# A head's 16 values on every other partition in a two-layer attention kernel: q, k and sums moved without filler, heads from chip to chip, the denominators alone by way of DRAM

## The chip, the cores and the metric

The kernel runs on one core of one Trainium2 chip. The metric is device microseconds (us) of one execution. The kernel before took 2535.94 us, the median of three runs (2533.43 to 2537.54).

The profile calls the engines PE (TensorE, matrix products; PEld is its loading of weights), DVE (VectorE), ACT (ScalarE), POOL (GpSimd) and SP (SyncE, which here only issues DMAs). The matrix engine writes to PSUM, which is divided into banks; the other on-chip memory is SBUF, with 128 partitions.

## The reference

The input x has the shape (2, 2048, 256), in fp32: 2 sequences of 2048 tokens. There are two layers of the same form, and both read the same normalized input:

```
xn = layernorm(x)
s  = attention(xn)              # layer 0: softmax over all 2048 keys; + xn
                                # layer 1: only keys with |i - j| <= 64
g  = silu(ffn(xn))              # layer 0: two branches of 8 low-rank experts
                                # layer 1: a product and 8 gated LoRA experts
x  = x + s * g
```

Each attention has 16 heads of 16 values:

```
q, k, v = split(xn @ w_qkv + b_qkv)
attn    = softmax(q k^T * scale)   # scale 1/16 in layer 0, 1/4 in layer 1
heads   = attn v
s       = heads @ w_o + b_o        # layer 0 adds xn
```

## The kernel before, in words

**Storage.** All activations are kept transposed: the 256 features lie on partitions, as 2 halves (NC = 2) of 128, and the tokens lie along the free dimension, worked on in blocks of TB = 512. So a sequence (batch b) has NB = 4 blocks. The 16 heads form NG = 4 groups g of four heads. One *item* of attention is (b, g, n): a sequence, a group of heads and a block of 512 queries; there are 32 items in each layer.

**Stages, by the trace.** Products of weights and the first layer norm (0 to 57 us), the router (to 124), the first feed-forward part (to 471), the keys, queries and values of layer 0 and the start of its attention (to about 597), the attention of layer 0 (to about 2124), then the layer norm, the second feed-forward part and the keys and queries of layer 1 (to about 2225), the values of layer 1 and the start of its attention (to 2290), its attention (to 2505) and a tail.

**Keys and queries by way of DRAM.** `keys_queries` (L473) writes k and q of a block into the DRAM tensor `qd` (L195), which has HP = 32 rows for each head: 16 rows of values and 16 rows of filler. The filler is written once near the start (L301 to L310): a tile of ones and a tile of zeros, each 128x512, go out in eight DMAs, so that the filler rows of k are ones and those of q are zeros. `fetch` (L581) reads one (b, g) of k and q back, 128 partitions by 2048 tokens each, so that head j of the group stands on partitions 32j to 32j + 31. Two k tiles and two q tiles take turns. In layer 1 the fetch is cut into two halves. `attention` begins with the fetch of the first two groups.

**Two passes over the scores.** `scores` (L596) issues both passes, for four heads side by side: each head uses 32 rows of PE (32x128 weights), so four heads fill its 128 rows.
- The first pass (`sq`, L667) makes q·k for the row maximum only; DVE reduces it (L679 in layer 0; L674 with the band's mask in layer 1).
- The negated maximum is then put into row 16 (HD) of each head of the q tile, where k has a one. In layer 0 `turn_max` and `fetch_max` do so through the DRAM tensor `md` on SP's queue. In layer 1 `place_max` transposes the maxima on PE, negates them on ACT (`row<-pmx`, L723) and issues `q<-row` on ACT's own queue (L726).
- The second pass (`sk`, L667) then yields q·k minus the maximum; ACT takes the exponential (L683), and in layer 1 POOL sets to zero what lies outside the band (L688).

**Weighing the values.** `values` (L526) makes v for 128 tokens at a time: two matmuls into a PSUM bank of a pool of six (`pp`, L541), then a copy into the tile `vs[b]`, by DVE for the first sequence, by ACT for the second. POOL has filled that tile with ones before (L514). A head has HV = 17 columns there: 16 values and a one that remains. `weigh` (L733) takes a window of 32 columns a head, so that the accumulator `acc` (L747) holds, on partition 32j + 16, the sum of the exponentials of head j: the softmax's denominator. In layer 0 ACT copies acc away and POOL adds it to `av` (L760, L761); in layer 1 ACT copies it into `av` (L752).

**After an item.** When its `av` (128x512) is complete, six steps follow, each a number of attention steps after the other (the `hops`, L867):
- `away` (L771): all of av, 256 KB, goes to the DRAM tensor `ad`.
- `compact` (L779): the denominators come back as `dn`, 128x16, and the heads, 128 KB, come back into xn, whose values are no longer needed (both read `ad`).
- `invert` (L785): DVE takes the reciprocal of dn.
- `write` (L788): dn goes to DRAM, `rd`.
- `spread` (L791): it comes back as `recb`, each denominator repeated on the 16 partitions of its head.
- `divide` (L798): the multiplication of heads and recb, on POOL; in layer 1 every second item on DVE.

The last item of layer 0 and the last four of layer 1 take another way without DRAM (`last_there` L805, `last_back` L819: transposes on PE). `project` (L830) follows when all four groups of a block are done. In xn the heads of a group stand as (value, head): partition 4d + j of the group's 64. To match this, the host permutes rows of w_o and the bias of v (`apart` in `_attn_arrays`, L1122).

**What sets the order.** The order of everything in attention is written out by hand, in steps. A step of layer 0 is one key block of 128 and one query block of 512 for four heads, there are 512 of them; a step of layer 1 is two query tiles of 128, there are 64. `after` is a table that says which functions follow which step, and the loop at L945 issues in each step: the second pass of step s together with the first pass of step s + U + LEAD, then jobs left from the values and keys of the second sequence, the weighing of an earlier step, and the functions of the table. `pin` (L698) keeps an instruction at its place in the program order of its engine. Before this loop stand, without pins, the memsets of the tiles (L514 to L523, all on POOL), the values of the first sequence (L545) and the fetches. All of SP's DMAs pass its one queue in order.

```
hops = (0, 1, 3, 4, 5, 7, 8) if local else (0, 2, 4, 5, 7, 11, 13)
...
for hop, f in zip(hops, steps):
    at(end + DEL + hop, f, i)
```

## Time and profile before

| | |
|---|---|
| median of three runs | 2535.94 us |
| the profiled execution | 2538.34 us |
| its span, on the profile's page | 2536.6 us |
| around the span | 1.74 us |
| mean TensorE clock granted | 0.999 |
| bytes of all DMAs | 129.83 MB in 146353 packets, of which 93456 under 512 B |
| read from and written to HBM | 80.50 MB and 45.97 MB |
| L679, DVE maxima of layer 0 | 1024, 1221 ns each |
| L674, DVE maxima of layer 1 | 512, 410 ns each on average |
| L683, ACT exponentials of layer 0 | 2048, 603 ns each |
| L761, POOL additions of layer 0 | 459, 1267 ns each |
| L771, DMAs away from av | 59 of 256 KB |
| L783 and L796, DMAs of heads and of reciprocals | 59 of 128 KB each |
| L589, fetches of k and q | 10 + 10 of 1024 KB, and halves in layer 1 |

The profile is of one execution, and its times are in us unless ns is written. A group's line gives the code line, the engine, the operation, what it writes and reads with shapes, and how often; after it come busy time, mean ns of one, and the engine's idle time before these instructions with what released it. "Chain" is the chain of work that ended last. Lines of a timeline begin with the start from the span's beginning and the length of a row of like instructions; in brackets stands the idle time before it and what ended it.

### The profile page before, as it was taken

How to read it: one execution, taken by the hardware profiler on the slowest of the kernel's cores; microseconds unless marked ns; L12 is line 12 of the kernel's file. 1: busy time of each engine (PE TensorE's matmuls, PEld its weight loads, DVE VectorE, ACT ScalarE, POOL GpSimd, SP SyncE). 2: the span in 40 equal slices, each digit the busy share in tenths (PEclk: the TensorE clock that was granted, in tenths of full speed). 3: DMA queues.
4: the chain of work that ended last, by engine and by line, in shares of the span. 5: the costliest groups of instructions: out<-in, count | busy, mean ns of one | idle time of the engine just before them, and what ended most of it. 6: DMA issues, size and time to landing. Idle time of an engine off the chain costs nothing.

```text
span 2536.6 us, 47898 instructions
## 1 busy us (share of the span) xinstructions
PE 2513.1 (99%) x18896; PEld 1060.6 (42%) x18896; DVE 1686.2 (66%) x2747; ACT 1620.8 (64%) x3187; POOL 876.6 (35%) x827
## 2 busy tenths in 40 slices
PE   8999999999999999999999999999999999999999
PEld 6444444444333333333333333333333334457766
DVE  4143333157888888888777788788888765238986
ACT  5400000126888888888888888888888886227755
POOL 0000000102444444444444444444444420016887
PEclk9999999999999999999999999999999999999999
DMA  6131111230001001001001001001000002133552
GB/s 243 50 84 51 52 51 39 82 118 14 14 14 43 16 12 44 16 12 44 16 12 43 10 18 44 12 17 43 15 14 10 14 14 63 49 133 108 163 167 81
DMA packets 146353, 129.83 MB, mean 51 GB/s; under 512 B 93456, under 2 KB 97936, under 8 KB 143568
## 3 DMA queue, kind: packets, MB, share of 16 engines
q1 hardware_dynamic: 144256, 125.46, 16.5%
q8 instruction: 148, 2.42, 0.4%
q10 hardware_dynamic: 1872, 1.31, 0.2%
q14 instruction: 77, 0.63, 0.1%
HBM read 80.50 MB, written 45.97 MB: 50 GB/s over the span
## 4 chain that ended last, share of the span: by engine, by line
PE 79%; DMA 1%; ACT 0%; POOL 0%; DVE 0%; issue 0%; ACTq 0%; SPq 0%; POOLq 0%; DVEq 0%
PE sk L667 25%; PE acc L747 22%; PE sq L667 19%; PE pp L477 5%; PE pr L835 2%; PE pp L532 2%; PE po L1027 1%; PE pt L1023 1%; PE po L1035 1%; PE xb L113 0%; PE xb L138 0%; DMA k<-qd 0%; PE of L827 0%; DMA q<-qd 0%; POOL xn L688 0%
## 5 line engine op out<-in xcount | busy, mean ns | idle before, releaser
L679 DVE TENSOR_REDUCE part<-sq 128x2 f32<-128x1024 f32 x1024 | 1207.3, 1221 | 294.3 <-PE sq L667 284.7
L683 ACT ACTIVATE e<-sk 128x512 f32<-128x512 f32 x2048 | 1058.3, 603 | 217.2 <-PE sq L667 197.7
L667 PE MATMUL sk<-q,k 32*128 32x512 f32 (+2 forms) x5632 | 1135.8, 533 | 1.2 <-ACT xn L683 1.0
L667 PE MATMUL sq<-k,q 32*128 32x512 f32 (+2 forms) x5120 | 1129.1, 569 | 0.5 <-DVE part L679 0.5
L761 POOL TENSOR_TENSOR av<-av,more 128x512 f32<-128x512 f32 x459 | 581.4, 1267 | 936.3 <-ACT more L760 931.1
L667 PEld LDWEIGHTS sk<-q,k 32*128 32x128 f32 x5632 | 522.0, 184 | 604.1 <-ACT e L683 512.5
L747 PE MATMUL acc<-e,v 128*32 128x512 f32 x4096 | 546.7, 605 | 0.0
L667 PEld LDWEIGHTS sq<-k,q 32*128 32x128 f32 x5120 | 402.3, 183 | 22.3 <-DVE part L679 13.2
L760 ACT COPY more<-acc 128x512 f32<-128x512 f32 x459 | 268.7, 585 | 1.2 <-PE acc L747 1.0
L747 PEld LDWEIGHTS acc<-e,v 128*32 128x32 f32 x4096 | 81.8, 108 | 388.2 <-ACT e L683 367.8
L461 ACT ACTIVATE gt<-po 128x512 f32<-128x512 f32 x16 | 8.8, 594 | 321.1 <-PE po L457 321.1
L674 DVE CUSTOM_DVE_ANT_0 seen<-sq,mask 128x256 f32<-128x256 f32 (+1 forms) x512 | 176.2, 410 | 53.6 <-PE sq L667 49.2
L467 POOL TENSOR_TENSOR x<-x,up 128x512 f32<-128x512 f32 x16 | 23.1, 1461 | 450.1 <-DVE up L464 277.5
L448 DVE TENSOR_TENSOR xs<-we,px 128x512 f32<-128x512 f32 x64 | 43.9, 686 | 136.2 <-PE px L440 130.3
L688 POOL TENSOR_SCALAR_AFFINE_SELECT xn<-xn 128x512 f32<-128x512 f32 x172 | 106.2, 652 | 77.4 <-ACT xn L683 75.7
L440 PE MATMUL px<-xn,FV 128*128 128x512 f32 x256 | 121.2, 595 | 0.0
L444 PE MATMUL py<-cum,FW 128*128 128x512 f32 x256 | 120.5, 593 | 0.6 <-DVE cum L412 0.6
L424 PE MATMUL po<-pr,UO 128*128 128x512 f32 x256 | 119.0, 592 | 0.0
L683 ACT ACTIVATE xn<-sk 128x512 f32<-128x512 f32 x172 | 89.8, 602 | 41.1 <-PE sk L667 17.9
L450 DVE TENSOR_TENSOR pr<-xs,py 128x512 f32<-128x512 f32 x64 | 44.0, 687 | 64.8 <-PE py L444 64.6
L424 PEld LDWEIGHTS po<-pr,UO 128*128 128x128 f32 x256 | 48.6, 190 | 61.2 <-issue 61.0
L444 PEld LDWEIGHTS py<-cum,FW 128*128 128x128 f32 x256 | 48.4, 190 | 61.5 <-issue 59.8
(195 smaller groups left out, 1604.0 us busy)
## 6 DMA issues: line engine op xcount, KB each, us to landing
we<-wd SPq DMA_DIRECT2D x128, 128.0 KB
ad<-av SPq DMA_DIRECT2D x59, 256.0 KB
qd<-sb SPq DMA_DIRECT2D x48, 256.0 KB
k<-qd SPq DMA_DIRECT2D x10, 1024.0 KB
q<-qd SPq DMA_DIRECT2D x10, 1024.0 KB
xn<-ad SPq DMA_DIRECT2D x59, 128.0 KB
recb<-rd SPq DMA_DIRECT2D x59, 128.0 KB
q<-qd SPq DMA_DIRECT2D x12, 512.0 KB
```

The costliest lines, as they stand in the source:

```text
L424: nc.tensor.matmul(po[oc], UO[:, ch, bass.ts(oc, P)], pr, start=(ch == 0), stop=False)
L440: nc.tensor.matmul(px, FV[:, c, bass.ts(ch, P)], xn[b][:, c, cols], start=(c == 0), stop=(c == NC - 1))
L444: nc.tensor.matmul(py, FW[:, c, bass.ts(ch, P)], cum[:, c, :], start=(c == 0), stop=(c == NC - 1))
L477: nc.tensor.matmul(ps, w[:, c, bass.ts(hf, P)], xn[b][:, c, bass.ts(n, TB)], start=(c == 0), stop=(c == NC - 1))
L667: nc.tensor.matmul(o, lhs, rhs, start=True, stop=True)
L674: nc.vector.tensor_tensor_reduce(seen[:, lo:hi], sq[:, d, t * 2 * P + lo : t * 2 * P + hi], mask[:, lo:hi], 1.0, LOWEST, ALU.add, ALU.max, ...
L679: nc.vector.tensor_reduce(pt[:, pair[0] : pair[1] + 1, t, kb], sq, AX.X, ALU.max)
L683: nc.scalar.activation(e, t, AF.Exp, scale=scale)
L688: nc.gpsimd.affine_select(out=e[:, :, c, :], in_=e[:, :, c, :], compare_op=ALU.is_ge, fill=0.0, base=0, pattern=[[0, 4], [sign, P]], chann ...
L747: nc.tensor.matmul(acc[hp[j], o : o + hi - lo], vs[b][:, kt, vcols(g, j)], es[j][:, lo:hi], start=(r == 0), stop=(r == len(parts) - 1), sk ...
L760: nc.scalar.copy(more, acc)
L761: nc.gpsimd.tensor_tensor(avs[i], avs[i], more, ALU.add)
```

## The change

A head's 16 values now stand on the even partitions of its 32, and what stood on partition 16 moves to an odd one: the maximum's row of q is partition 31 (HP - 1) of each head, and the denominator is on partition 15 (DEN).

- `qd` holds 16 rows a head and no filler; the eight DMAs of filler and the tile of zeros are gone. `fetch` reads 64 rows into every second partition, half the bytes.
- The filler is made in SBUF: DVE sets both k tiles (2048 columns in layer 0, 2176 in layer 1) to one and both q tiles (2048 columns) to zero at the beginning of each attention.
- The first pass uses 31 rows a head, without the maximum's row; the second pass still 32.
- The copy of the values writes every second column of a head's window; the odd columns of the window are written by its two neighbours, except one, column 15, which keeps its one and gives the denominator on partition 15.
- `away` moves only the four denominators' rows, 8 KB. The heads no longer pass DRAM: `compact` moves them straight from av (every second partition) to xn, so av is released there, and no longer by `away`.
- dn is 32x64 instead of 128x16, and `rd` is read with the head as its outermost dimension (4) instead of the value (16).
- The heads stand in xn as (head, value), so `last_there` and `last_back` change their layout and the host no longer permutes w_o and the bias.

The instructions of PE keep their order and number, and so do the steps and hops.

```
+DEN = HD - 1
...
-        [2, B, H, HP, T], F32, name="qd"
+        [2, B, H, HD, T], F32, name="qd"
...
-        zeros = fw.tile([P, TB], F32, name="zeros")
-        nc.vector.memset(zeros, 0.0)
-        for b in range(B):
-            for i, t in ((0, ones), (1, zeros)):
-                for half in range(NC):
-                    nc.sync.dma_start(
-                        out=qd[i, b, bass.ts(half, H // NC), HD:, :], in_=t[:, None, :].to_broadcast([P, NB, TB])
-                    )
...
+            for k, q in zip(ks, qs):
+                nc.vector.memset(k, 1.0)
+                nc.vector.memset(q, 0.0)
             for t in vs:
                 nc.gpsimd.memset(t, 1.0)
...
+                s = vs[b][p0:p1, c, :]
                 copy(
-                    vs[b][p0:p1, c, : H * HV].rearrange("p (h w) -> p h w", w=HV)[:, :, :HD],
+                    bass.AP(s.tensor, s.offset, [s.ap[0], [HV, H], [2, HD]]),
                     ps[p0:p1, :].rearrange("p (h w) -> p h w", w=HD),
                 )
...
+            hq = [slice(j * HP, (j + 1) * HP - 1) for j in range(NG)]
...
-                    nc.sync.dma_start(out=t[:, to], in_=qd[i, b, bass.ts(g, NG), :, s].rearrange("h w t -> (h w) t"))
+                    nc.sync.dma_start(out=t[::2, to], in_=qd[i, b, bass.ts(g, NG), :, s].rearrange("h w t -> (h w) t"))
...
-                                        q1[hp[j], bass.ts(qt, P)], k1[hp[j], qt * P + lo : qt * P + hi],
+                                        q1[hq[j], bass.ts(qt, P)], k1[hq[j], qt * P + lo : qt * P + hi],
...
-                    out=q[HD:P:HP, bass.ts(n, TB)].rearrange("j (t c) -> j t c", c=P), in_=row
+                    out=q[HP - 1 : P : HP, bass.ts(n, TB)].rearrange("j (t c) -> j t c", c=P), in_=row
...
-                pin(nc.sync.dma_start(out=ad[i % 3].rearrange("j w f -> (j w) f"), in_=avs.pop(i)))
+                pin(nc.sync.dma_start(out=ad[i % 3], in_=avs[i][DEN::HP]))
...
-                return d.rearrange("j (r e) -> r j e", r=P // NG)
+                return d.rearrange("j (r e) -> (j r) e", e=DE)
...
-                divs[i] = op.tile([P, NG * TB // P], F32, name="dn", tag="dn", bufs=3)
-                pin(nc.sync.dma_start(out=divs[i], in_=flat(ad[i % 3][:, HD, :])))
-                pin(nc.sync.dma_start(out=together(*items[i]), in_=ad[i % 3][:, :HD, :].rearrange("j d f -> d j f")))
+                divs[i] = op.tile([NG * TB // DE, DE], F32, name="dn", tag="dn", bufs=3 if local else 1)
+                pin(nc.sync.dma_start(out=divs[i], in_=flat(ad[i % 3])))
+                pin(nc.sync.dma_start(out=together(*items[i]), in_=avs.pop(i)[::2]))
...
-                pin(nc.sync.dma_start(out=divs[i], in_=rd[i % 3][None, :, :].to_broadcast([HD, NG, TB])))
+                pin(nc.sync.dma_start(out=divs[i], in_=rd[i % 3][:, None, :].to_broadcast([NG, HD, TB])))
```

More of the change, by code (lines that the diff above doesn't have):

```diff
@@ L481, in keys_queries @@
         nc.scalar.activation(sb, ps, AF.Identity, bias=bias[:, hf : hf + 1])
-        nc.sync.dma_start(out=qd[i, b, bass.ts(hf, H // NC), :HD, bass.ts(n, TB)], in_=sb)
+        nc.sync.dma_start(out=qd[i, b, bass.ts(hf, H // NC), :, bass.ts(n, TB)], in_=sb)
     def attention(A, scale, local, final, start=None, projected=False):
@@ L501, in attention @@
         LEAD = 3 if local else 6
+        DE = 64
         DEL = 2 if local else 1
@@ L508, in attention @@
             ks = [kq.tile([P, T + 2 * PAD], F32, name=f"k{i}", tag=f"k{i}") for i in range(2)]
-            ad = [dr.tile([NG, HP, TB], F32, name=f"ad{i}", tag=f"ad{i}") for i in range(3)]
+            ad = [dr.tile([NG, TB], F32, name=f"ad{i}", tag=f"ad{i}") for i in range(3)]
             rd = [dr.tile([NG, TB], F32, name=f"rd{i}", tag=f"rd{i}") for i in range(3)]
             md = [dr.tile([NG * TT, P], F32, name=f"md{i}", tag=f"md{i}") for i in range(2)]
+            for k, q in zip(ks, qs):
+                nc.vector.memset(k, 1.0)
+                nc.vector.memset(q, 0.0)
             for t in vs:
@@ L663, in scores @@
                                 pieces.append((
-                                    when, sq[:, d], q1[hp[j], bass.ds(n1 * TB + t * P, P)], k1[hp[j], bass.ts(kb, TB)]
+                                    when, sq[:, d], q1[hq[j], bass.ds(n1 * TB + t * P, P)], k1[hq[j], bass.ts(kb, TB)]
                                 ))
@@ L709, in fetch_max @@
                 pin(nc.sync.dma_start(
-                    out=tiles(i)[0][HD:P:HP, bass.ts(items[i][2], TB)],
+                    out=tiles(i)[0][HP - 1 : P : HP, bass.ts(items[i][2], TB)],
                     in_=md[i % 2].rearrange("(j t) p -> j (t p)", t=TT),
@@ L810, in last_there @@
                     nc.tensor.transpose(ps[:, t].rearrange("p j w -> p (j w)"), av[:, bass.ts(t, P)], ident)
-                rec = op.tile([P, TT, NG], F32, name="dn", tag="dn", bufs=3)
-                o = divs[i] = op.tile([P, TT, HD, NG], F32, name="over", tag="recb", bufs=2)
-                nc.vector.reciprocal(rec, ps[:, :, :, HD])
+                rec = op.tile([P, TT, NG], F32, name="rec", tag="rec", bufs=2)
+                o = divs[i] = op.tile([P, TT, NG, HD], F32, name="over", tag="recb", bufs=2)
+                nc.vector.reciprocal(rec, ps[:, :, :, DEN])
                 nc.vector.tensor_tensor(
-                    o.rearrange("p t d j -> p t j d"), ps[:, :, :, :HD],
-                    rec[:, :, :, None].to_broadcast([P, TT, NG, HD]), ALU.mult,
+                    o, ps[:, :, :, ::2], rec[:, :, :, None].to_broadcast([P, TT, NG, HD]), ALU.mult
                 )
@@ L822, in last_back @@
                 lo = g % 2 * NG * HD
-                o = divs.pop(i).rearrange("p t d j -> p t (d j)")
+                o = divs.pop(i).rearrange("p t j d -> p t (j d)")
                 ps = pm.tile([P, TB], F32, name="of", tag="m")[lo : lo + NG * HD, :]
@@ L1122, in _attn_arrays @@
 def _attn_arrays(l, wq, wk, wv, bq, bk, bv, wo_t, bo):
-    apart = lambda m: m.reshape(NG, NG, HD, -1).transpose(0, 2, 1, 3).reshape(m.shape)
     cols = lambda v: np.asarray(v).reshape(NC, P).T
@@ L1129, in _attn_arrays @@
         f"wv{l}": wv,
-        f"wo{l}": apart(np.asarray(wo_t).T),
+        f"wo{l}": np.asarray(wo_t).T,
         f"bq{l}": cols(bq),
         f"bk{l}": cols(bk),
-        f"bv{l}": cols(apart(np.asarray(bv))),
+        f"bv{l}": cols(bv),
         f"bo{l}": cols(bo),
```

## The prediction

> **What bounds the kernel now.** I read the page's busy times and its chain first, then the busy time by stage, then the order of time at the two places where the change puts something new.

> ```profile
> span 2536.6 us, 47898 instructions
> PE 2513.1 (99%) x18896; PEld 1060.6 (42%) x18896; DVE 1686.2 (66%) x2747; ACT 1620.8 (64%) x3187; POOL 876.6 (35%) x827
> PE 79%; DMA 1%; ACT 0%; POOL 0%; DVE 0%; issue 0%; ACTq 0%; SPq 0%; POOLq 0%; DVEq 0%
> ```

> TensorE is idle for 23.5 us of the span and carries the chain. A busy PE can still be a slow PE, so I took the spacing of the acc groups of L747: in layer 0, 455 of some 500 steps are 2.92 or 2.93 us apart. A step holds three groups of eight matmuls (sk, sq, acc), each about 1 us. That is PE's own pace, not another engine's. By stage:

> ```profile
> 1200.00:1500.00 300.00, 300.00 (x2371) 101.87 (x2364) 237.80 (x222) 247.85 (x488) 133.06 (x105) 1.00 0.08 19
> 2225.00:2290.00 65.00, 64.17 (x281) 39.86 (x281) 21.84 (x99) 17.37 (x34) 9.63 (x10) 1.00 0.39 130
> 2290.00:2400.00 110.00, 108.25 (x2130) 86.60 (x2133) 98.10 (x553) 82.13 (x184) 88.56 (x138) 1.00 0.46 142
> 2400.00:2505.00 105.00, 103.20 (x1810) 75.92 (x1806) 85.62 (x444) 67.90 (x155) 88.18 (x126) 1.00 0.46 142
> ```

> Columns after the length: PE, PEld, DVE, ACT, POOL, then clock, DMA share, GB/s. Layer 0 leaves PE no idle time and DMA nearly none to do. In layer 1 (from 2290) PE is idle for 1.75 and 1.8 us only, but DVE is at 89% and DMA at 46%. So a transfer saved can bring back at most 3.55 us there, and DVE is the engine nearest to taking over. Before it, from 2225, lies a stretch in which PE fills PSUM banks that DVE must empty.

> **The change, part by part.**

> *The eight fills and the zeros tile.* They issue from 33.5 to 67 us. SP's next transfer is at 116.4, PE waits for a DMA only once early (4.7 us, before the fills), and it is busy for 63.00 of the 63 us after 64. I take 0; with no such cover, 0.5 us of gain.

> *Memsets of k and q, layer 0.* They go between the two last up steps at 470.9 (L464). DVE's next work is the first copy of values at 501.71, after 29.4 us of idle time, and some 9 us of memsets fit. Behind the second up waits POOL's add, then POOL's two memsets of v (474.70, 7.8 us); 2 us later is still before 501. I take 0.

> *The same memsets, layer 1.* Here there is no such gap.

> ```profile
> 2224.44 1.61 DVE L1041 SCALAR_TENSOR_TENSOR x<-gt,bo,x 128x512 f32<-128x512 f32 x2 [4.23 <-ACT gt L1039]
> 2224.75 8.27 POOL L515 MEMSET v<- 128x4879 f32 x2 [91.76 <-PE po L1035]
> 2225.32 15.23 PE L532 MATMUL pp<-wv,xn 128*64 128x256 f32 x68 [0.69 <-ACT gt L1039]
> 2228.95 2.43 DVE L535 COPY v<-pp 64x256 f32<-64x256 f32 x6 [2.89 <-POOL v L515]
> 2231.81 0.43 DVE L535 COPY v<-pp 128x256 f32<-128x256 f32 x1 [0.44 <-PE pp L532]
> ```

> PE runs 17 groups of values 0.865 us apart and has six banks. The six copies that wait for POOL until 2228.95 are just in time: the seventh group began at about 2231.8 - 0.9 = 2230.9 and needs the first copy's bank. In the changed program DVE does: x step, memset k (2176 columns), x step, memset q (2048), k, q, and only then the copies. The first k waits for PE's last po, so it starts near 2225.2. The rest is 0.8 us of x step and 8448 columns. What does a column cost?

> ```profile
> 1.27 0.48 DVE L302 MEMSET ones<- 128x512 f32 x1
> 1.82 0.48 DVE L305 MEMSET zeros<- 128x512 f32 x1
> ```

> The row says 485 ns for 512 columns, and with the mask's 272 ns for 256 that is 0.83 ns a column. The starts lie 0.55 us apart, 1.07 ns a column. [...] By the row the memsets take 7.0 us, the first copy ends at 2225.2 + 0.8 + 7.0 + 0.4 = 2233.4 and PE stands for 2.5 us. [...] I take 4.3, since starts show what the next instruction waits for. After it the copies run at 0.4 us against 0.865, so no second stall; but PE is full until 2290, so nothing gives the 4.3 back. [...] The trace's clock is 1.00 in every stage after the first, so I take 0 and keep 1.7 for the range.
> The fetches of k and q (SP) now wait for these memsets, until about 2227 to 2235 instead of 2224.7; they are half as large and first used at 2248. Behind them on SP is nothing until 2243.9. 0.

> *The first pass on 31 rows.* The tile stays 32x128 at the same place. The nearest row is L457 with 16 rows: 587 ns at least, like the 592 of the 128-row matmuls with 512 columns. I take 0. Each 10 ns a step would be 5 us, so this is a rival.

> *The reciprocal on 32x64 instead of 128x16, 59 times.*

> ```profile
> L786 DVE RECIPROCAL dn<-dn 128x16 f32<-128x16 f32 x59 | 14.4, 244 | 0.2
> L191 DVE RECIPROCAL rec_r<-mx_r 128x32 f32<-128x32 f32 x2 | 0.7, 354 | 0.1
> L191 DVE RECIPROCAL rec_g<-mx_g 128x16 f32<-128x16 f32 x2 | 0.5, 253 | 0.1
> ```

> 16 further columns cost 101 ns, so 64 columns cost 354 + 202 = 556 ns, 0.31 us more. In layer 0 (31 of them) DVE has 19% idle time: 0. In layer 1 (28) an item is 6.50 us of PE; DVE needs 16 x 0.344 + 0.25, and in every second item 0.85 for the division: 5.75 or 6.6 us, with 0.31 more 6.1 or 6.9. At one such item (2458) DVE left the second pair's bank 0.06 us before PE wrote it, so 0.25 us is lost. Fourteen items divide on DVE, four of them beside projections with room: 10 x 0.15 = 1.5 us taken; bounds 0 and 14 x 0.31 = 4.3.

> *Smaller transfers, layer 1.* Per item 256 KB out and 128 KB back become 8 KB out and 128 KB on the chip; fetches are halved. What they cost now:

> ```profile
> 2467.25 0.26 ACT L723 ACTIVATE row<-pmx 16x128 f32<-16x128 f32 x1
> 2468.87 0.54 ACTq L726 DMA_DIRECT2D q<-row  x1
> ```

> ACT held its queue for 1.3 us behind a fetch issued at 2463.97, and PE's acc came 1.18 us late. All layer 1 steps beyond 6.50 us an item add up to 2.5 us. I take -2.0; bounds -3.55 (all PE idle time) and 0. The later release of av (after the heads' move) has three buffers, 19.5 us, against some 11 us: 0.

> *The spread of the reciprocals.* Its source loses 16 as its outermost dimension and gets 4. [...] The write ahead of it lands sooner behind smaller fetches, so I take 0.

> *SP in layer 0.* The write of the maxima loses its wait for PE (16 waits, 6.4 us in all), but 9.94 to 11.08 us lie between its two DMAs, mostly the first one's landing. Six steps are late by 3.6 us in all. I take 0, bound -3.6. The away, compact and spread steps run tens of us ahead of need: 0.

> **Sum.** 4.3 + 1.5 - 2.0 = +3.8. The profiled execution took 2538.34 us (span 2536.6, 1.7 around it), so 2542.1 for such a one; it stands 2.4 above the median 2535.94, so against the median 2539.7, said as 2540. About 0.2%, 5.1 us, is what a measurement can tell from none.

> **Rivals.**
> - *Transfers were worth more* (faster). Layer 1's 3.55 us and layer 0's 3.6 all come back, the stall is only 2.5, the reciprocal hides: -4.7, 2531. For it: every such wait passes SP or a fetch. Against: layer 0's waits are for an unchanged DMA. Chance 0.13.
> - *DVE takes over layer 1* (slower). Once DVE's item is longer than PE's 6.50 us, each of the 14 dividing items passes on its 0.31 us, and PE's late start hides the transfers' gain: 4.3 + 4.3 = +8.6, 2544.5. For it: DVE's 89%. Against: items without a division have 0.4 us of room to catch up. Chance 0.28.
> - *The change does not do what it says: 31 rows cost.* If the four heads no longer ran side by side, eight matmuls of 0.59 us would replace a 1.07 us group, milliseconds in all. Chance 0.03.
> - The likeliest, 0.56: 2537 to 2543.

> It lies within 0.2% (up to 2541.0) in about three quarters and above in a quarter; 0.02 of each of the first two rivals ends within too. So same is 0.42 + 0.04 = 0.46, slower 0.14 + 0.26 + 0.03 = 0.43, faster 0.11. The range takes in the first rival's inner part and the clock beside the second: 2533 to 2548.

> **What would show it.** Right: sq groups as long as before and steps of 2.92; four DVE memsets ahead of the first v copy near 2234, with a gap of 3 to 5 us inside the values; reciprocals near 556 ns; no held q<-row at the fetches. Wrong: a gap under 2 us, layer 1 items well off 6.50 us, or a clock below 1.00 after the gap.

## The result and the profile after

The changed kernel takes 2544.94 us, the median of seven runs (2542.17 to 2548.56), beside 2536.73 us for the kernel before in seven runs (2532.11 to 2539.51). The ratio is 1.0035 with a 95% interval of 1.0025 to 1.0045: slower by some 8.9 us by the ratio; the two medians lie 8.2 us apart. That lies inside the range of the prediction, but above its likeliest case.

The head of the page of the changed kernel:

```profile
span 2543.5 us, 47862 instructions
PE 2517.2 (99%) x18896; PEld 1062.1 (42%) x18896; DVE 1716.5 (67%) x2754; ACT 1622.9 (64%) x3187; POOL 877.8 (35%) x827
DMA packets 119829, 89.68 MB, mean 35 GB/s; under 512 B 81160, under 2 KB 85640, under 8 KB 118324
```

The bytes moved fell from 129.83 to 89.68 MB, and PE's idle time rose from 23.5 to 26.3 us. But PE's busy time rose as well, by 4.1 us, with the same 18896 matmuls. That is a first hint of a slower clock somewhere. The same stages as before (length, busy times of PE, PEld, DVE, ACT and POOL, clock, DMA share, GB/s):

```profile
1200.00:1500.00 300.00, 300.00 (x2368) 102.40 (x2364) 238.79 (x221) 247.50 (x486) 132.95 (x105) 1.00 0.05 11
2225.00:2290.00 65.00, 60.32 (x257) 36.89 (x257) 24.77 (x87) 16.00 (x29) 7.80 (x10) 0.97 0.28 98
2290.00:2400.00 110.00, 108.68 (x2037) 85.98 (x2036) 99.33 (x542) 80.10 (x179) 83.68 (x131) 1.00 0.23 71
2400.00:2505.00 105.00, 104.42 (x1792) 76.31 (x1793) 91.81 (x462) 66.48 (x151) 86.67 (x126) 1.00 0.26 85
```

The second row is the boundary: PE's idle time went from 0.83 to 4.68 us, and the clock from 1.00 to 0.97. In layer 1 DMA is half as busy, DVE more, and PE counts as idle for 1.90 us instead of 3.55 although the stage takes longer: its waits for DVE apparently lie within its groups of matmuls and are not counted there, an inference from these two numbers and the longer items below. There the spacing of the items has to be read, not the busy time.

For the place of the time I took, from PE's order of time in both traces, the start of the first instruction of each kind:

| stretch | before | after | difference |
|---|---|---|---|
| start to the first product of the router (L329, L321) | 57.36 | 54.72 | -2.64 |
| to the first keys of layer 0 | 413.96 | 413.96 | 0.00 |
| to the first values of layer 1 | 1754.00 | 1754.82 | +0.82 |
| to the keys of the second sequence | 15.74 | 21.87 | +6.13 |
| to the first sq of layer 1 | 7.07 | 7.06 | -0.01 |
| to the first transposition of the tail | 253.92 | 256.51 | +2.58 |
| to the end of the span | 34.55 | 34.56 | +0.01 |

The sum is the 6.9 us between the two spans. The -2.64 us at the start is not the change's: two executions of the kernel before differ there by as much (last section). Without it the change costs +9.5 us in this pair of traces, of which 6.1 us lie in the values of layer 1, 2.6 us in its attention and 0.8 us in layer 0.

**The boundary.** The order of time there:

```profile
2222.93 8.27 POOL L512 MEMSET v<- 128x4879 f32 x2 [91.73 <-PE po L1032]
...
2223.50 5.59 PE L529 MATMUL pp<-wv,xn 128*64 128x256 f32 x24 [0.69 <-ACT gt L1036]
2223.78 1.87 DVE L509 MEMSET k<- 128x2176 f32 x1 [0.40 <-DVE x L1038]
...
2226.57 1.76 DVE L510 MEMSET q<- 128x2048 f32 x1 [0.38 <-issue]
...
2228.74 1.87 DVE L509 MEMSET k<- 128x2176 f32 x1 [0.40 <-issue]
...
2230.98 1.76 DVE L510 MEMSET q<- 128x2048 f32 x1 [0.37 <-issue]
...
2232.78 2.70 DVE L533 COPY v<-pp 64x256 f32<-64x256 f32 x7
2233.26 10.19 PEld L529 LDWEIGHTS pp<-wv,xn 128*128 128x128 f32 x40 [4.58 <-DVE v L533]
2233.26 11.60 PE L529 MATMUL pp<-wv,xn 128*128 128x256 f32 x44 [4.17 <-DVE v L533]
```

PE fills its six banks with 24 matmuls (four in each) and stands for 4.17 us, until the first copy. The four memsets and the x step between them take from 2223.78 to 2232.78. Then 44 matmuls take 11.60 us; at the pace of before (15.23 us for 68) they would take 9.86. So 1.74 us more are lost behind the gap. PE's granted clock in short stretches says why (length, PE busy, clock, DMA share, GB/s):

```profile
2229.10:2233.20 4.10, 0.00 (x0) 1.00 0.71 204
2233.20:2234.20 1.00, 0.94 (x3) 0.72 0.75 246
2234.20:2236.20 2.00, 2.00 (x6) 0.50 0.60 221
2236.20:2237.20 1.00, 1.00 (x4) 0.58 0.12 49
2237.20:2238.20 1.00, 1.00 (x6) 1.00 0.00 0
```

The clock is halved for some 3.4 us after PE starts again (3.41 us in the record of the clock, from 2233.63 on).

**Layer 1.** The reciprocals and divisions on DVE from 2290 to 2510:

```profile
L784 DVE RECIPROCAL dn<-dn 32x64 f32<-32x64 f32 x27 | 14.5, 536 | 0.2
L800 DVE TENSOR_TENSOR xn<-xn,recb 64x512 f32<-64x512 f32 x12 | 10.3, 862 | 0.5 <-DMA recb<-rd 0.3
```

A reciprocal went from 246 to 536 ns. Where it hurts is an item that also divides on DVE; one of these, in the kernel before and in the changed one:

```profile
2401.66 0.90 DVE L802 TENSOR_TENSOR xn<-xn,recb 64x512 f32<-64x512 f32 x1
2402.49 0.23 DVE L786 RECIPROCAL dn<-dn 128x16 f32<-128x16 f32 x1
2402.65 0.35 DVE L674 CUSTOM_DVE_ANT_0 seen<-sq,mask 128x256 f32<-128x256 f32 x1
```

```profile
2407.24 0.90 DVE L800 TENSOR_TENSOR xn<-xn,recb 64x512 f32<-64x512 f32 x1
2408.07 0.53 DVE L784 RECIPROCAL dn<-dn 32x64 f32<-32x64 f32 x1
2408.53 0.35 DVE L673 CUSTOM_DVE_ANT_0 seen<-sq,mask 128x256 f32<-128x256 f32 x1
```

From the start of the division to the next read of scores it is 0.99 us before and 1.29 us after. DVE has no idle time around it (in the changed kernel none from 2404.83 to 2413.99), so the 0.30 us reach PE. The time of an item (from the start of the transposition pmx of the item before to that of its own, us; items counted from 0; all others are the same within 0.05 us but for item 24, 6.60 before and 6.37 and 6.36 in the others):

| item | 9 | 11 | 13 | 15 | 17 | 19 | 25 | 27 | 29 | 31 |
|---|---|---|---|---|---|---|---|---|---|---|
| before | 6.72 | 6.54 | 6.78 | 6.41 | 6.72 | 6.35 | 6.59 | 7.43 | 6.79 | 5.37 |
| after | 7.02 | 6.65 | 7.07 | 6.70 | 7.02 | 6.64 | 7.71 | 6.64 | 7.08 | 6.16 |
| after, dn 128x16 (experiment a_dn128) | 6.73 | 6.55 | 6.79 | 6.42 | 6.72 | 6.35 | 7.41 | 6.44 | 6.79 | 5.38 |

### The profile page after: what moved, and what is told of

The parts are those of the page before. It is cut to its first block, busy times and chain, and to the rows that moved or that the text cites. A ratio compares the mean times of both kernels' runs of the same rounds, so it can differ in the third digit from the quotient of the medians.

```text
span 2543.5 us, 47862 instructions
## 1 busy us (share of the span) xinstructions
PE 2517.2 (99%) x18896; PEld 1062.1 (42%) x18896; DVE 1716.5 (67%) x2754; ACT 1622.9 (64%) x3187; POOL 877.8 (35%) x827
## 2 busy tenths in 40 slices
DMA packets 119829, 89.68 MB, mean 35 GB/s; under 512 B 81160, under 2 KB 85640, under 8 KB 118324
## 4 chain that ended last, share of the span: by engine, by line
PE 80%; DVE 1%; ACT 1%; issue 0%; POOL 0%; ACTq 0%; POOLq 0%; DVEq 0%
PE sk L666 25%; PE acc L746 22%; PE sq L666 19%; PE pp L469 5%; PE pr L832 2%; PE pp L529 2%; PE po L1024 1%; PE pt L1020 1%; PE po L1032 1%; PE xb L114 0%; PE xb L139 0%; ACT xn L682 0%; PE pmx L719 0%; PE of L824 0%; POOL xn L687 0%
## 5 line engine op out<-in xcount | busy, mean ns | idle before, releaser
L666 PE MATMUL sq<-k,q 31*128 31x512 f32 (+2 forms) x5120 | 1130.6, 569 | 0.5 <-DVE part L678 0.5
L666 PEld LDWEIGHTS sq<-k,q 31*128 31x128 f32 x5120 | 402.8, 183 | 24.0 <-DVE part L678 13.2
```

Of the source, the lines that this page charges most:

```text
L666: nc.tensor.matmul(o, lhs, rhs, start=True, stop=True)
```

## The experiments

They ran in three groups, each with the kernel before timed on the same chip. That kernel's median was 2539.28, 2543.82 and 2544.64 us in them, so only ratios are compared across groups. The theory: the boundary costs 6.1 us (a gap and a slower clock after it) and the reciprocals some 3 us, and the smaller transfers bring nothing in layer 1. Rivals: layer 1 absorbs what is repaired at the boundary, or the later landing of recb (in layer 0 a median of 3.47 us behind the issue, against 2.44 before) makes the items long.

| run | median, us | ratio to before, 95% interval |
|---|---|---|
| a_q_act | 2542.09 | 1.0010 (1.0003 to 1.0016) |
| a_q1_act | 2545.99 | 1.0032 (1.0020 to 1.0044) |
| a_dn128 | 2546.09 | 1.0025 (1.0014 to 1.0036) |
| b_memsets | 2549.59 | 1.0039 (1.0026 to 1.0051) |
| a_best | 2539.64 | 0.9982 (0.9974 to 0.9990) |
| a_best_lead7 | 2544.85 | 0.9999 (0.9991 to 1.0007) |
| b_lead7 | 2548.70 | 1.0017 (1.0010 to 1.0024) |
| b_dn32 | 2544.23 | 1.0002 (0.9993 to 1.0010) |
| a_best_again | 2543.27 | 0.9992 (0.9984 to 1.0000) |
| after_again | 2553.83 | 1.0037 (1.0024 to 1.0050) |

The kernels a_half and before_again were executed once each, for the trace (2545.57 and 2544.95 us).

**a_q_act: q's memsets of layer 1 on ACT.**

```
-                nc.vector.memset(q, 0.0)
+                if local:
+                    nc.scalar.activation(q, x[0][:, 0, :], AF.Copy, scale=0.0)
+                else:
+                    nc.vector.memset(q, 0.0)
```

> The changed kernel, but in layer 1 ACT, which is idle there, sets the two q tiles to zero (a copy of x times 0), so that DVE has only the two memsets of k ahead of the copies of the values. Theory (the boundary carries most of the loss: 4.2 us in which PE stands and 1.7 us after it at a lower clock): the first copy starts within 0.5 us of where POOL's memset of v lets it start, PE has no gap in the values, the clock stays at 1.00, and the time falls by 5 to 6.5 us, to about 2539. Rival (layer 1 is bound by DVE, and work that starts earlier only waits later): the gap goes but the time falls by less than 3 us.

Its order of time at the boundary:

```profile
2227.31 3.70 ACT L511 ACTIVATE q<-x 128x2048 f32<-128x2048 f32 x2
2227.47 15.39 PE L532 MATMUL pp<-wv,xn 128*64 128x256 f32 x68 [0.69 <-ACT gt L1039]
2227.74 1.87 DVE L509 MEMSET k<- 128x2176 f32 x1 [0.40 <-DVE x L1041]
```

All 68 matmuls run in one row of 15.39 us, and the stretch is 0.16 us longer than before instead of 6.13. The ratio fell from 1.0035 to 1.0010, some 6.3 us, and the two intervals do not overlap. From its first sq to the tail layer 1 takes 255.94 us, against 256.51 in the changed kernel: it absorbs nothing of what was gained.

**b_memsets: the four memsets alone, in the kernel before.**

```
+            for k, q in zip(ks, qs):
+                nc.vector.memset(k, 1.0)
+                nc.vector.memset(q, 0.0)
             for t in vs:
                 nc.gpsimd.memset(t, 1.0)
```

> The kernel before with the four memsets of k and q on DVE added at the start of each attention, which the fetches then overwrite wholly: extra work that changes no result. Theory: PE has a gap of about 4.2 us in the values of layer 1 and a granted clock near 0.57 for 4 us after it; the time rises by 5.5 to 6.5 us. Rival (in the kernel before, the larger fetches that then start later cost more, or the stall is partly taken up by waits later in layer 1): the rise is over 8 us or under 4 us.

The gap is 4.17 us again, and the stretch 7.31 us longer, since here the clock stayed at half for about 5.8 us behind the gap (last section; in after_again as well, 7.28 us longer). Ratio 1.0039, some 9.9 us with an interval from 6.6: more than the boundary, on the side of the rival, but its layer 1 is not longer (the last pmx follows the first after 221.36 us, 221.76 in the first trace of the kernel before). By the trace the rest lies in layer 0 (1758.89 us, against 1754.00), which differs from execution to execution (below).

**a_q1_act and a_half: how long must the gap be?** The first moves one memset of q to ACT, the second all but 1024 columns of one q (shown).

```
-                nc.vector.memset(q, 0.0)
+                if local and q is qs[0]:
+                    nc.scalar.activation(q, x[0][:, 0, :], AF.Copy, scale=0.0)
+                elif local:
+                    nc.scalar.activation(q[:, 1024:], x[0][:, 0, 1024:], AF.Copy, scale=0.0)
+                    nc.vector.memset(q[:, :1024], 0.0)
+                else:
+                    nc.vector.memset(q, 0.0)
```

> The changed kernel with one of the four memsets of layer 1 (that of the second q tile) moved from DVE to ACT. PE's gap should shrink by that memset's 2.2 us, from 4.2 to about 2 us. If the lower clock needs an idle time of over some 3 us, it stays at 1.00 after the gap and the time falls by 2.2 + 1.7 = 3.9 us; if the clock's loss goes in proportion to the idle time, the clock still falls for about 2 us and the time falls by about 3.0 us; if the gap has nothing to do with the clock, by 2.2 us.

> The changed kernel with three quarters of the zeroing of q in layer 1 on ACT: DVE does both memsets of k and 1024 columns of one q. PE's gap in the values should be about 1.0 us (2.03 us with one whole memset of q more, none with none). With a gap of 2.03 us the clock fell as far and as long as with 4.17 us. If any gap of about a microsecond starts the fall, the values after it take 1.7 us longer again; if it needs one to two microseconds, they do not, and the stage is only 1.0 us longer than without a gap.

PE's row after the gap and its clock, for a_q1_act:

```profile
2233.38 11.60 PE L532 MATMUL pp<-wv,xn 128*128 128x256 f32 x44 [2.03 <-DVE v L536]
```

```profile
2231.30:2233.40 2.10, 0.07 (x2) 1.00 0.85 308
2233.40:2234.40 1.00, 1.00 (x5) 1.00 0.75 188
2234.40:2237.40 3.00, 3.00 (x9) 0.53 0.39 145
2237.40:2238.40 1.00, 1.00 (x4) 0.71 0.00 0
```

and for a_half:

```profile
2236.19 9.91 PE L535 MATMUL pp<-wv,xn 128*128 128x256 f32 x44 [0.97 <-DVE v L539]
```

```profile
2235.20:2236.20 1.00, 0.03 (x2) 1.00 0.57 238
2236.20:2237.20 1.00, 1.00 (x5) 1.00 0.59 66
2237.20:2240.20 3.00, 3.00 (x16) 1.00 0.81 325
```

A gap of 2.03 us costs the same 3.4 us at half clock as one of 4.17 us (11.60 us for the 44 matmuls in both), and the fall comes 1.2 us after PE has started again. A gap of 0.97 us costs nothing more than itself. The stretch of a_q1_act is 3.99 us longer than before, 2.03 of gap and the rest the clock. Against the changed kernel that is 2.14 us less, the number set down for a gap that has nothing to do with the clock (2.2 us). That it fits is luck: the clock did fall, as far and as long as with the longer gap. The two other cases set down, a gap of over some 3 us being needed and a loss in proportion to the gap, are excluded. The ratio of a_q1_act, 1.0032, is higher than the 1.0027 that this gives, but within its interval.

**a_dn128: dn as 128x16 again.**

```
-        DE = 64
+        DE = 16
```

> The changed kernel with dn as 128x16 again instead of 32x64 (nothing else). Theory (DVE is the bound in the items that divide on it, and each longer reciprocal is passed on there): reciprocals near 250 ns, the six items that are 0.29 us longer than in the kernel before become as long as before, and the time falls by 1.8 to 2.8 us. Rival (the reciprocal hides, and the longer items come from the later landing of recb): the items stay 0.29 us longer and the time falls by less than 0.8 us.

Reciprocals take 246 ns, and the items are as in the table above: the ten listed are 3.1 us shorter together than in the changed kernel. Ratio 1.0025, some 2.5 us less than 1.0035; the intervals overlap, so the time alone does not show it, and the items do. In this kernel recb is still read with 4 as the outermost dimension, and its layer 1 takes 221.40 us against 221.36 (b_memsets) and 221.76 (before) with 16: with 4 recb lands later in the changed kernel (3.47 us behind the issue against 2.44 in layer 0, next section), but that costs nothing here.

**b_dn32: the longer reciprocals alone, in the kernel before.**

```
-                return d.rearrange("j (r e) -> r j e", r=P // NG)
+                return d.rearrange("j (r e) -> j r e", e=64)
...
-                divs[i] = op.tile([P, NG * TB // P], F32, name="dn", tag="dn", bufs=3)
+                divs[i] = op.tile([NG * TB // 64, 64], F32, name="dn", tag="dn", bufs=3 if local else 1)
```

> The kernel before with dn as 32x64 instead of 128x16 (the longer reciprocals alone, 256 KB and 128 KB transfers as before). Theory (DVE-bound items pass the 0.29 us on): seven or eight items of layer 1 are 0.2 to 0.3 us longer, together 2.3 to 3.1 us, ratio 1.0010 to 1.0012. Rival (they are longer only with the smaller transfers, or because of the spread with 4 as its outermost dimension): no item longer than in the kernel before, within 0.5 us.

By the trace the items 9, 13, 17 and 29 are 0.28 to 0.31 us longer, without the smaller transfers, which excludes the rival. Layer 1 as a whole is 6.3 us longer, though, not 2.3 to 3.1: items 15 and 19 stand out, with 0.9 and 3.6 us. In item 19 ACT's queue is held for 2.1 us ahead of q<-row, behind a fetch of q:

```profile
2409.77 0.26 ACT L723 ACTIVATE row<-pmx 16x128 f32<-16x128 f32 x1
2412.16 0.54 ACTq L726 DMA_DIRECT2D q<-row  x1
2412.80 1.08 ACT L683 ACTIVATE xn<-sk 128x512 f32<-128x512 f32 x2 [2.77 <-DMA q<-qd]
```

PE stands for 1.95 us for want of the exponentials, and its clock is half for 3.41 us from 2414.68 on, which costs 1.7 us more. The traced execution is the slowest of the 13. The time of all, 1.0002 with an interval up to 1.0010, is lower than the theory says and cannot confirm the size; it stays with the items.

**a_best and a_best_again: both repairs,** the diffs of a_q_act and a_dn128 together.

> The changed kernel with both repairs: ACT sets the q tiles of layer 1 to zero, and dn is 128x16. Theory (the boundary and the longer reciprocals carry all of the loss, and the smaller transfers are worth nothing because none of them was on the path): the time is that of the kernel before within 0.1%, that is, minus 0.4 us in layer 1 and plus 0.2 us at the boundary. Rival (the smaller transfers are worth the 2 us of the prediction and the two costs hid it): 2 to 3.5 us below the kernel before, ratio 0.9990 or less.

> The changed kernel with both repairs (q tiles zeroed on ACT in layer 1, dn 128x16), once more on what may be another chip: its ratio of 0.9982 to the kernel before was 4.6 us lower than the traces' layer 1 and boundary explain (0.2 us). If the smaller transfers shorten layer 0's late steps, the ratio is 0.9990 or less again, and the late steps add up to 1 to 4 us less than in the repeated kernel before; if that ratio belonged to that chip alone, it is within 0.9993 to 1.0005.

> The changed kernel, once more, timed beside the repaired one on one chip. If the two repairs are worth 6.1 and 3.1 us as the traces say, the repaired one is 8 to 10.5 us faster than this one; this one is at 1.0025 to 1.0045 of the kernel before, with a gap of 4.2 us in the values and clock 0.5 for some 3.4 us after it.

On one chip the changed kernel took 2553.83 us and the repaired one 2543.27, 10.6 us apart: the two repairs undo all of the loss. Both runs of the repaired kernel are below the kernel before, by 0.18% and 0.08%, the second with an interval that reaches 1. Layer 1 and the boundary don't explain that: its layer 1 takes 221.40 and 221.41 us, as above. What is left is layer 0.

**before_again, and the late steps of layer 0.**

> The kernel before, once more, for a trace from the same chip as the three others of this group. Late steps of layer 0 (those over 3.05 us that no projection explains) add up to 9 us or more if the earlier traces of the kernel before with edits (9.2, 9.4, 10.5 us) are the rule, and to 4 us if the first trace (3.6 us) is.

From the first keys of layer 0 to the first values of layer 1, two executions of the same kernel take 1754.00 and 1763.28 us, on different chips. A part of that are late steps, which come at different items each time. Another part is the clock: it is half for 3.41 us at the keys of layer 0 in most traces, and for 3.41 or 6.83 us at the end of its attention (2111 to 2128 us) in all but the first pair. In the table what is left is the stretch without the late steps and without half of PE's time at the half clock (us; at the boundary of the changed kernel 3.41 us of it cost 1.74; the kernels with LEAD 7 are left out):

| timed together | trace | transfers | stretch | late steps | at half clock | left |
|---|---|---|---|---|---|---|
| first pair | before | large | 1754.0 | 3.6 | 3.4 | 1748.7 |
| | after | small | 1754.8 | 3.8 | 3.4 | 1749.3 |
| group 1 | b_memsets | large | 1758.9 | 7.0 | 6.8 | 1748.8 |
| | a_q_act | small | 1756.4 | 5.4 | 3.4 | 1749.4 |
| | a_q1_act | small | 1758.2 | 6.0 | 6.8 | 1749.2 |
| | a_dn128 | small | 1757.6 | 5.0 | 6.8 | 1749.3 |
| group 2 | b_dn32 | large | 1762.9 | 9.5 | 10.2 | 1748.7 |
| | a_best | small | 1759.9 | 8.7 | 3.4 | 1749.5 |
| group 3 | before_again | large | 1763.3 | 9.9 | 10.2 | 1748.7 |
| | after_again | small | 1763.1 | 8.2 | 10.2 | 1750.3 |
| | a_best_again | small | 1760.5 | 7.7 | 6.8 | 1749.4 |
| | a_half | small | 1761.0 | 8.1 | 6.8 | 1749.7 |

In each group but the first pair the kernels with the smaller transfers were shorter in this stretch, but by the late steps and the clock; what is left is 0.4 to 1.6 us longer. So the regular steps of layer 0 did not become faster. The late steps may have become fewer, as set down for a_best_again, but one trace for each kernel doesn't show it, nor which transfer would bring it. The time of a_q_act leaves nothing for such a gain: its 2.5 us are the 0.2 of its boundary and the 2.2 to 2.6 by which its layer 1 is longer than with the short reciprocals.

**a_best_lead7 and b_lead7: one step more between the passes.**

```
-        LEAD = 3 if local else 6
+        LEAD = 3 if local else 7
```

> The same kernel with LEAD 7 instead of 6 in layer 0: the first pass, and with it the maxima's way through DRAM, begins one step of 2.93 us earlier. The late steps of layer 0 (3.6 to 7.1 us in all, 0.3 to 2.2 us each, different ones in each execution) are put down to the second pass waiting for the maxima, whose write to DRAM lands some 10.5 us after its issue. If so, they all go, the time falls by 3.5 to 7 us against the kernel without it, to a ratio of about 0.998 to the kernel before, and the runs scatter less. Rival (they come from the clock or another DMA): they stay, and the time is the same within 1 us.

> The kernel before with LEAD 7 in layer 0, nothing else. By the same reason 3.5 to 7 us less than before, ratio about 0.998, with late steps gone; this says whether what the late steps cost has anything to do with the change. Rival: the same within 1 us.

Both became slower, by 0.17% each. The late steps stayed (10.4 and 10.6 us). They moved from the 15th to the 14th accumulation of an item, that is, they kept their place in the first pass. So they are not the second pass waiting for the maxima: that theory is wrong. The part ahead of the first accumulation grew as well, to 130.7 us, from 126.6 to 128.4 in all other traces. In five of the six late steps of the changed kernel's trace a reduction on DVE starts late, waiting for PE, in the last 1.1 us before the write of the maxima lands (seen by SP's issue of q<-md); what links the two I did not find.

## Why the prediction was right and wrong

- **Fills, memsets of layer 0, 31 rows: right at 0.** The stretch up to the first keys of layer 0 behind the start is 413.96 us in both, and the one from there to the first acc, which holds the memsets, 128.33 us before and 128.37 us after. A matmul sq takes 569 ns on average with 31 rows as with 32, and the usual step of layer 0 went from 2.925 to 2.927 us on average: 0.8 us over the 473 such steps, in every trace with the change and in none without it. What makes it is open.
- **Memsets of layer 1: mechanism right, size too small.** The gap was predicted at 4.3 us and is 4.17, in part by luck. No run shows the 4.3, the author's estimate: it needs 8.8 us for the 8448 columns, and the trace shows 8.0 in their place, by the starts of the memsets without the x step; but the first starts 0.28 us behind PE's first matmul of the values instead of 0.12 ahead of it, and the x step takes 1.01 us, not 0.8. A column is 0.95 ns, halfway between the 1.07 of the starts of ones and zeros and the row's 0.83; the row lacked the 0.4 us between two memsets. The term that failed is "I take 0 and keep 1.7 for the range": no run shows the 1.7, an estimate of the author's as well, and in its place the clock took 1.74 us, and 2.9 in two other traces. The reason given for the 0 was a misreading. A clock of 1.00 in every stage is a mean, and hid a fall that the trace of the kernel before does hold, at the keys of layer 0, behind 3.41 us in which PE was idle for 1.17 (length, PE busy, clock, DMA share, GB/s):

```profile
468.29:471.70 3.41, 2.24 (x7) 1.00 0.00 0
471.70:475.11 3.41, 3.41 (x5) 0.50 0.02 5
```

So the clock fell in the kernel before as well, and the change made the gap at the boundary.

- **Reciprocals: 1.5 us predicted, 3.1 measured.** The length was right (556 ns predicted, 536 measured). The failed step is that an item loses 0.15 us on average, "10 x 0.15". Seven items lost 0.28 to 0.30 us each, as the second rival says, and others 0.1, 0.2 and 0.8 (item 31, where a_q_act lost 0.2); around a division DVE has no idle time to catch up with.
- **Smaller transfers: -2.0 predicted, 0 measured in layer 1.** The wait that I counted, an ACT queue held behind a fetch, is real, and with the large transfers it comes in most traces: 1.36 us in item 27 of the kernel before (7.43 us), 0.95 us in item 19 of before_again, 2.12 us in item 19 of b_dn32, up to 0.38 us in b_lead7, none in b_memsets. With the small transfers it is 0.45 to 0.91 us, at item 25, in all eight traces with LEAD 6 and in the one with LEAD 7. The failed step is that such a wait is lost to the whole stage. Where item 27 or 19 is held, item 25 is shorter (6.59 us in before and in before_again, 7.41 us in b_memsets), and with short reciprocals layer 1 takes 221.36 to 221.76 us in four traces with the large transfers and 221.40 to 221.48 us in four with the small ones. Only in b_dn32 was the wait not made good. PE's idle time in a DVE-bound stage wasn't DMA's to give back.
- **The spread: right at 0, though recb lands later.** In layer 0 the last update of the semaphore that tells of its landing comes a median of 2.44 us behind the issue in the kernel before (16 updates) and 3.47 us in the changed one (5 updates), 1.0 us later. In layer 1 four divisions of the kernel before start less than 5 us after the issue, the shortest 4.37 us (2456.56 to 2460.93). In the changed kernel the shortest time is 4.40 us, and one division on DVE waits 0.3 us for the landing.
- **SP in layer 0: right at 0** within what the traces separate. Between the two DMAs of the maxima lie 9.97 to 11.27 us after the change, as before.

The sum is then 6.1 + 3.1 + 0 = 9.2 us against 3.8 predicted and 8.9 measured. The second rival had nearly the number (+8.6), but by luck: its reciprocals were too large (4.3) and its boundary, without the clock, too small (4.3), and the two errors cancel.

## What to carry to other kernels

Before a new instruction is put on an engine at a stage's boundary, count how many buffers the next engine can fill meanwhile; here six banks are 5.6 us, and 9 us of memsets went in front. The gaps of 4.17 and 2.03 us that were made anew in TensorE's work were paid twice here, once as idle time and once as a slower clock behind it (half for 3.4 us or more); the one of 0.97 us was paid once. So an idle engine is worth using (ACT's two copies take 3.70 us, two memsets of q on DVE 3.5). A mean clock of 1.00 over a stage does not say that the clock never fell in it (at the keys of layer 0 it was 0.50 for 3.41 us): look at stretches of a few us behind each gap. When an engine is at 89% in a stage, look for the items in which it has no idle time: here the longer reciprocal counted in full in seven of them (0.28 to 0.30 us each), and the smaller transfers counted nothing.

## What the runs showed of the hardware

```profile
2235.04:2238.45 3.41, 0.21 (x1) 1.00 0.99 382
2238.45:2241.86 3.41, 2.44 (x6) 0.50 1.03 418
2241.86:2245.27 3.41, 3.41 (x10) 0.50 0.56 226
2245.27:2248.68 3.41, 3.41 (x18) 1.00 0.02 5
```

So one and the same gap cost 1.7 or 2.9 us at the clock, where it lay differently on the grid: it ended 0.37 us ahead of the end of a step in the changed kernel and 0.97 us behind one in b_memsets. How much idle time a step must hold for a fall is not settled: 1.94 us (b_dn32) and 2.03 us (a_q1_act) were enough, 1.75 us (the kernel before, 2110.09 to 2113.51) and 0.97 us (a_half) were not, but the fall at the keys of layer 0 came behind a step with only 1.17 us.

The start of the kernel differs too. The kernel before and its repetition, eight equal matmuls in each:

```profile
8.97 3.78 PE L251 MATMUL psf<-wk,wiT 128*128 128x256 f32 x8 [0.52 <-DVE aq L256]
```

```profile
9.12 1.99 PE L251 MATMUL psf<-wk,wiT 128*128 128x256 f32 x8 [0.52 <-DVE aq L256]
```

In the first they take nearly twice as long, and the router then begins at 57.36 instead of 54.90 us. The record of the clock begins only behind them in the first (14.31 us) and at 8.55 us in the repetition, so that a half clock there is inferred from the lengths. In all 14 traces the two go together: the router begins at 56.8 to 57.6 us where the record begins at 13.0 to 14.5 us, and at 53.6 to 54.9 us where it begins at 8.0 to 9.1 us (the changed kernel: 54.72 and 8.14 us). So two single traces of this kernel can differ by 2.5 us before anything that was changed.
